# Sobel layers of a four-layer network: products in column halves with 128 rows, and another pipeline order

## The chip, the cores and the metric

The kernel runs on one core of one Trainium2 chip. The metric is the device time of one execution in microseconds (us), lower being better. A core has five engines with a queue each: TensorE (PE in the profile, with its weight loads as PEld), VectorE (DVE), ScalarE (ACT), GpSimd (POOL) and SyncE (SP). Each works its own queue in order and waits at semaphores for the others. SBUF is the working memory of 128 partitions; PSUM[...] takes the products of TensorE.

## The reference

The input `x` has shape (1, 256, 256, 32): height, width, channels, all float32. Four layers are added to it one after the other, each on the group-normed value:

```python
x = x + L0(_gn(x), ...)   # layer norm, then a gated projection
x = x + L1(_gn(x))        # Sobel layer
x = x + L2(_gn(x))        # Sobel layer, the same once more
x = x + L3(_gn(x), ...)   # recurrent cell, 256 steps along the width
```

`_gn` subtracts the mean and divides by the standard deviation over height, width and the two channels of each of 16 groups. A Sobel layer is

```python
pooled = _avg_pool3_same(x)        # 3 x 3 mean over the positions that exist
grad_x = _depthwise3(pooled, kx)   # difference along width, smoothed along height
grad_y = _depthwise3(pooled, ky)   # difference along height, smoothed along width
return jnp.sqrt(grad_x * grad_x + grad_y * grad_y + 1e-6)
```

with Sobel kernels divided by 4 and the same for every channel.

## The kernel before

**Layout.** `xa` and `xb` hold the whole image in SBUF. A partition is a width position inside a group of four times a channel (4 x 32 = 128), the free axis is 64 such groups (`NB`) times 256 heights (`S`). Everything along height is then elementwise work on shifted rows; everything along width is a product with a fixed 128x128 matrix on TensorE. A Sobel layer goes through 32 blocks of two groups (`NST = 32`), so 128 x 512 numbers at a time. The first Sobel layer reads `xa` and writes `xb`, the second goes back.

**One block.** `normalize` (L413, ACT) writes the normed block twice, as `xp` in PSUM and as `xn` in SBUF. `twos` (L420, DVE) adds neighbouring rows to `u`. `threes` (L429, DVE) adds the third row, into `pp`, which is padded by a zero row at each end; `ends` (L423, ACT) writes its two border rows. `fours` (L434, DVE) adds neighbours of `pp` to `v`. `smooth` (L438, POOL) adds neighbours of `v` to `sh`, the smoothed value along height; `difference` (L442, POOL) subtracts rows of `pp` that lie two apart, giving `dh`. Both are rings of eight groups, four blocks deep.

Pooling and Sobel along width together reach two width positions to each side. So a group of four needs itself and half a group on each side. `kt` holds five 128x128 matrices for each of the two gradients: from the group before, from itself, from the group after, and from itself for the first and the last group. `centre` (L449, L459 for the two end blocks) multiplies by the matrix of the group itself; `edges` (L489) adds what comes from the group before (rows 64 to 127 of the ring into columns 0 to 63 of the output) and from the group after (rows 0 to 63 into columns 64 to 127), as 64x64 products. Where the ring wraps, a product of 512 columns is cut in two of 256. Gradient 1 takes `dh`, gradient 0 takes `sh`; they land in the PSUM tiles `pg1` and `pg0`.

`square` (L495, ACT) squares both, gradient 1 in place and gradient 0 into `sq`; `total` (L499, DVE) adds them to `ss`; `root` (L503, ACT) takes the root, back into the PSUM tile of gradient 1; `residual` (L506, DVE) adds the input; `statistics` (L509, DVE) collects the statistics for the next group norm.

**Order.** Nothing here is scheduled by a planner. Each part has a time in a list, `parts`, block k is shifted by `every * k`, the whole list is sorted, and the instructions are emitted in that order. So the times set only the order within each engine's queue; when an instruction starts is up to its queue and its semaphores. Tiles rotate: three PSUM tiles for each gradient, two for `xp`, two SBUF tiles each for `xn`, `u`, `v`, `sq`, `ss`, and two fixed `pp`.

**Beside it.** After the statistics of the first blocks one piece of preparation for the last layer is put in (`between`): in the first Sobel layer reductions on DVE (L641, L645) and 24 subtractions on POOL (L648), in the second a few small products that borrow a `pg1` tile (L660, L669, L675). After each layer `group_norm` (L155 to L174) finishes the statistics, with filler products on TensorE (`junk`, L145). Other lines named below: L333 to L349 belong to the first layer's gate and output projection, L710 to the last layer's preparation, L900 and above to the recurrence.

Of the kernel before, what the change touches and what calls it, by code (L numbers as in the profile page):

```python
# [11 lines left out]
F32 = mybir.dt.float32  # L12
BF16 = mybir.dt.bfloat16
AF = mybir.ActivationFunctionType
# [4 lines left out]
S = 256  # L19
# [3 lines left out]
NB = T // J  # L23
P = 128
# [9 lines left out]
K_GN, K_CEN, K_AVG, K_SOBEL = 0, 1, 2, 3  # L34
# [26 lines left out]
def net_kernel(  # L61
# [20 lines left out]
    nc = tc.nc  # L82
# [15 lines left out]
    kt = cp.tile([P, NK, P], F32, name="kt")  # L98
# [34 lines left out]
    NST = NB // 2  # L133
# [51 lines left out]
    for g in range(4):  # L185
        rows = slice(g * C, (g + 1) * C)
# [9 lines left out]
    with tc.tile_pool(name="nat", bufs=3) as natp, tc.tile_pool(  # L196
        name="ps_in", bufs=4, space=PSUM
    ) as ps_in:
        norm_test(tc, natp, flag, gn_gamma, gn_beta)
        for w0 in range(0, T, WL):  # L200
# [3 lines left out]
            for b2 in range(WL // (2 * J)):  # L204
# [10 lines left out]
                dst = xa[:, blk : blk + 2, :].rearrange("p b s -> p (b s)")  # L215
# [15 lines left out]
    def pair(t, k):  # L231
        return t[:, 2 * k : 2 * k + 2, :].rearrange("p b s -> p (b s)")

    with tc.tile_pool(name="ln", bufs=4) as lnp:
        rstd = lnp.tile([P, 2 * S], F32, name="rstd", bufs=1)
        with tc.tile_pool(name="ps_ln", bufs=6, space=PSUM) as ps_ln, tc.tile_pool(
            name="ps_var", bufs=1, space=PSUM
# [38 lines left out]
        with tc.tile_pool(name="ps_sp", bufs=8, space=PSUM) as ps_sp:  # L276
            for i, (k, g, ks) in enumerate(pairs):
                rows = slice(g * C, (g + 1) * C)
# [3 lines left out]
                    lhsT=spread[rows, ks * J : (ks + 1) * J, :].rearrange("p j c -> p (j c)"),  # L282
                    rhs=rstd[rows, :],
                    start=True,
                    stop=True,
# [19 lines left out]
    with tc.tile_pool(name="at", bufs=3) as atp, tc.tile_pool(  # L305
        name="ps_g", bufs=4, space=PSUM
# [72 lines left out]
    RING = 8  # L379
    Q = P // 2  # L380

    def sobel_layer(src, dst, scale, bias, between):

        stats = new_stats()
        stack = ExitStack()
        kp = stack.enter_context(tc.tile_pool(name="sobk", bufs=1))
        sp = stack.enter_context(tc.tile_pool(name="sob", bufs=2))
        ps_s = stack.enter_context(tc.tile_pool(name="ps_s", bufs=3, space=PSUM))
        ps_c = stack.enter_context(tc.tile_pool(name="ps_c", bufs=2, space=PSUM))

        along = [kp.tile([P, RING, S], F32, name="sh"), kp.tile([P, RING, S], F32, name="dh")]

        pps = [kp.tile([P, 2, S + 2], F32, name=f"pp{i}") for i in range(2)]
        for pp in pps:
            nc.gpsimd.memset(pp[:, :, 0 : S + 2 : S + 1], 0.0)
        v = {}

        def flat(t):
            return t.rearrange("p b s -> p (b s)")

        def ring(k):
            b = 2 * k % RING
            return slice(b, b + 2)

        def normalize(k):
            for key, t in (
                ("xp", ps_c.tile([P, 2, S], F32, name="xp")),
                ("xn", sp.tile([P, 2, S], F32, name="xn")),  # L410
            ):
                v[key, k] = t
                nc.scalar.activation(  # L413
                    flat(t), pair(src, k), AF.Identity, scale=scale, bias=bias
                )

        def twos(k):
            u = v["u", k] = sp.tile([P, 2, S - 1], F32, name="u")
            xn, xp = v.pop(("xn", k)), v["xp", k]
            nc.vector.tensor_add(u, xn[:, :, 0 : S - 1], xp[:, :, 1:S])  # L420

        def ends(k):
            nc.scalar.mul(  # L423
                pps[k % 2][:, :, 1 : S + 1 : S - 1], v["u", k][:, :, 0 : S - 1 : S - 2], 1.5
            )

        def threes(k):
            u, xp = v.pop(("u", k)), v.pop(("xp", k))
            nc.vector.tensor_add(pps[k % 2][:, :, 2:S], u[:, :, 0 : S - 2], xp[:, :, 2:S])  # L429

        def fours(k):
            pp = pps[k % 2]
            w = v["v", k] = sp.tile([P, 2, S + 1], F32, name="v")
            nc.vector.tensor_add(w, pp[:, :, 0 : S + 1], pp[:, :, 1 : S + 2])  # L434

        def smooth(k):
            w = v.pop(("v", k))
            nc.gpsimd.tensor_add(along[0][:, ring(k), :], w[:, :, 0:S], w[:, :, 1 : S + 1])  # L438

        def difference(k):  # L440
            pp = pps[k % 2]
            nc.gpsimd.tensor_sub(along[1][:, ring(k), :], pp[:, :, 0:S], pp[:, :, 2 : S + 2])  # L442

        def centre(k, which):
            pg = v["pg", which, k] = ps_s.tile([P, 2, S], F32, name=f"pg{which}")
            k0 = K_SOBEL + 5 * which
            b = 2 * k % RING
            if 0 < k < NST - 1:
                nc.tensor.matmul(  # L449
                    flat(pg),  # L450
                    lhsT=kt[:, k0 + 1, :],
                    rhs=flat(along[which][:, ring(k), :]),
                    start=True,
                    stop=False,
                )
                return
            for i in range(2):
                m = 3 if 2 * k + i == 0 else 4 if 2 * k + i == NB - 1 else 1
                nc.tensor.matmul(  # L459
                    pg[:, i, :],  # L460
                    lhsT=kt[:, k0 + m, :],
                    rhs=along[which][:, b + i, :],
                    start=i == 0,
                    stop=False,
                )

        def edges(k, which):

            pg = v["pg", which, k]
            k0 = K_SOBEL + 5 * which  # L470
            sides = []
            for m, first, rows, cols in (
                (0, 2 * k - 1, slice(Q, P), slice(0, Q)),
                (2, 2 * k + 1, slice(0, Q), slice(Q, P)),
            ):
                blocks = [(n, n - first) for n in (first, first + 1) if 0 <= n < NB]
                parts = []
                if len(blocks) == 2 and (first + 1) % RING:
                    b = first % RING
                    parts.append((flat(along[which][rows, b : b + 2, :]), flat(pg[cols])))  # L480
                else:
                    for n, i in blocks:
                        parts.append((along[which][rows, n % RING, :], pg[cols, i, :]))
                sides.append([(kt[rows, k0 + m, cols], rhs, out) for rhs, out in parts])
            while any(sides):
                for side in sides:
                    if side:
                        w, rhs, out = side.pop(0)
                        nc.tensor.matmul(out, lhsT=w, rhs=rhs, start=False, stop=not side)  # L489

        def square(k, which):
            pg = flat(v["pg", which, k])
            sq = pg if which else sp.tile([P, 2 * S], F32, name="sq")
            v["sq", which, k] = sq
            nc.scalar.activation(sq, pg, AF.Square)  # L495

        def total(k):
            ss = v["ss", k] = sp.tile([P, 2 * S], F32, name="ss")
            nc.vector.tensor_add(ss, v.pop(("sq", 0, k)), v["sq", 1, k])  # L499

        def root(k):
            mag = v["mag", k] = v.pop(("sq", 1, k))
            nc.scalar.activation(mag, v.pop(("ss", k)), AF.Sqrt, bias=sobel_eps)  # L503

        def residual(k):
            nc.vector.tensor_add(pair(dst, k), pair(src, k), v.pop(("mag", k)))  # L506

        def statistics(k):
            nc.vector.bn_stats(stats[:, k, :], pair(dst, k))  # L509

        every = 4.0
        parts = [
            (-1.45, normalize, ()),
            (0.0, twos, ()),
            (0.66, ends, ()),
            (0.66, threes, ()),
            (1.32, fours, ()),
            (1.4, difference, ()),
            (2.05, smooth, ()),
            (2.6 + 4.0, centre, (1,)),  # L520
            (3.46 + 4.0, centre, (0,)),
            (0.3 + 8.0, edges, (1,)),
            (1.35 + 8.0, edges, (0,)),
            (1.5 + 8.0, square, (1,)),
            (2.5 + 8.0, square, (0,)),
            (3.2 + 8.0, total, ()),
            (0.0 + 12.0, root, ()),
            (1.98 + 12.0, residual, ()),
            (2.6 + 12.0, statistics, ()),
        ]  # L530
        todo = [
            (k * every + when, k, part, args) for k in range(NST) for when, part, args in parts
        ]
        todo.sort(key=lambda e: e[:2])
        with tc.manual_schedule():
            for _, k, part, args in todo:
                part(k, *args)
                if part is statistics and between:
                    between.pop(0)(lambda: flat(ps_s.tile([P, 2, S], F32, name="pg1")))
        stack.close()  # L540
        return stats
# [202 lines left out]
class RecurrentInputs:  # L744
# [33 lines left out]
    def of(self, t, rows):  # L778
# [12 lines left out]
        m=0.300, sq=1.814, rd=1.883, pw=2.686, tg=4.187, sf=4.207, so=4.930, fc=5.023,  # L791
# [3 lines left out]
        m=4.328, sq=5.425, rd=6.234, pw=8.247, sf=8.370, tg=8.501, si=8.549, fc=8.711,  # L795
# [297 lines left out]
```

## Time and profile before

| What | us |
|---|---|
| Median of three runs (2629.62 to 2633.8) | 2632.47 |
| The profiled execution, its own time | 2632.46 |
| Its span in the trace, first to last instruction | 2630.6 |
| First Sobel layer, first `xp` to end of the last statistics | 326.0 to 469.9 |
| Second Sobel layer, the same | 475.3 to 617.65 |
| Busy in the span: PE / DVE / ACT / POOL | 2574.9 / 2329.4 / 2296.4 / 1298.0 |

The page gives for each engine its busy time and for each group of instructions the count and mean. The timeline lists single instructions: start, duration, engine, line, operation, the tile written and those read, the shape; in brackets the idle time before it and what ended it. A product in float32 shows up as two records, each with its weight load. Two instructions of one engine may overlap in the trace, since the next one starts while the last one drains; so what an instruction costs in a full queue is the distance of starts, not the duration.

### The profile page before, as it was taken

The page shows a single profiled execution, that of the slowest core. Times are in us where ns is not written, and L with a number is a line of the kernel's source. Part 1 is how long each engine was busy: PE and PEld are TensorE (multiplying, and loading weights), DVE is VectorE, ACT ScalarE, POOL GpSimd, SP SyncE. Part 2 cuts the span into 40 slices and gives each one's busy share as a digit, 9 for nine tenths or more (in the row PEclk, how much of TensorE's full clock was granted, in tenths as well). Part 3 has the DMA queues.
Part 4 walks back from the last instruction along what each step waited for, and adds up shares of the span by engine and source line. Part 5 has one row for each costly group of instructions (what it writes and reads, how often), then busy time and mean ns, then how long its engine had stood idle before and what let it go on. Part 6 is the DMA issues. An engine that isn't in the chain of part 4 may idle for free.

```text
span 2630.6 us, 43062 instructions
## 1 busy us (share of the span) xinstructions
PE 2574.9 (98%) x11181; PEld 1007.4 (38%) x11181; DVE 2329.4 (89%) x6735; ACT 2296.4 (87%) x6948; POOL 1298.0 (49%) x1288
## 2 busy tenths in 40 slices
PE   7999999998999999999999999999999999999997
PEld 4533433433333333333333333333333333333332
DVE  6788799796999999999999999999999999999996
ACT  5677677675999999999999999999999999999996
POOL 2211276463555555555555555555555555555553
PEclk9899999999999999999999999999999999999998
DMA  4000000002010000001010101010000001000000
GB/s 146 1 1 1 18 1 1 0 1 49 1 25 8 18 12 14 16 10 20 6 21 5 21 5 21 5 24 9 18 12 14 16 10 20 6 5 5 5 5 10
DMA packets 110744, 38.68 MB, mean 15 GB/s; under 512 B 74852, under 2 KB 107653, under 8 KB 110488
## 3 DMA queue, kind: packets, MB, share of 16 engines
q1 hardware_dynamic: 108452, 34.54, 6.1%
q8 instruction: 92, 1.51, 0.3%
q14 instruction: 164, 1.34, 0.2%
q10 hardware_dynamic: 1236, 0.99, 0.1%
q0 software_dynamic: 800, 0.30, 0.1%
HBM read 10.63 MB, written 8.39 MB: 7 GB/s over the span
## 4 chain that ended last, share of the span: by engine, by line
PE 93%; DVE 3%; ACT 2%; POOL 1%; issue 1%; DMA 1%; DVEq 0%; SPq 0%; ACTq 0%; POOLq 0%
PE zz L911 35%; PE zz L906 16%; PE zz L879 8%; PE pt L963 6%; PE pv L315 5%; PE pg L489 4%; PE pg L449 3%; PE zz L876 3%; PE pg L339 2%; PE pt L959 2%; PE pg L315 1%; PE px L1008 1%; PE pc L259 1%; PE px L998 1%; PE pb L280 1%
## 5 line engine op out<-in xcount | busy, mean ns | idle before, releaser
L927 POOL TENSOR_TENSOR rs<-ve,mhalf 128x4 f32<-128x4 f32 x1024 | 1047.1, 1023 | 953.5 <-DVE ve L924 953.5
L911 PE MATMUL zz<-wc,hT 128*128 128x512 f32 x2040 | 1069.0, 612 | 1.4 <-DVE hT L969 1.2
L900 ACT ACTIVATE ga<-zz,rs 128x128 f32<-128x128 f32 x3072 | 974.7, 376 | 53.6 <-POOL rs L927 47.3
L924 DVE TENSOR_REDUCE ve<-sq 128x4 f32<-128x516 f32 x1024 | 705.2, 689 | 69.4 <-ACT sq L919 49.1
L919 ACT ACTIVATE sq<-zz 128x512 f32<-128x512 f32 x1024 | 623.7, 609 | 53.8 <-PE zz L911 14.2
L906 PE MATMUL zz<-wc,hT 128*128 128x512 f32 x1024 | 524.4, 594 | 0.0
L911 PEld LDWEIGHTS zz<-wc,hT 128*128 128x128 f32 x2040 | 306.7, 189 | 355.8 <-DVE hT L969 168.7
L900 ACT ACTIVATE go<-zz,rs 128x128 f32<-128x128 f32 x1024 | 394.1, 385 | 0.0
L947 DVE TENSOR_TENSOR c<-ga 128x128 f32<-128x128 f32 x1024 | 298.4, 291 | 65.1 <-ACT ga L900 58.6
L951 DVE TENSOR_TENSOR fc<-ga,c 128x128 f32<-128x128 f32 x1020 | 297.9, 292 | 5.5 <-ACT ga L900 4.1
L955 DVE TENSOR_TENSOR c<-c,fc 128x128 f32<-128x128 f32 x1020 | 286.7, 281 | 8.8
L879 PE MATMUL zz<-fx,xt 32*128 32x512 f32 x2048 | 265.8, 589 | 0.0
L333 DVE TENSOR_TENSOR o<-pv,sg 128x512 f32<-128x512 f32 x256 | 158.1, 681 | 43.3 <-PE pg L315 37.7
L959 PEld LDWEIGHTS pt<-ident,go 128*128 128x128 f32 x512 | 71.1, 139 | 290.8 <-ACT go L900 283.4
L906 PEld LDWEIGHTS zz<-wc,hT 128*128 128x128 f32 x1024 | 172.7, 209 | 9.4 <-issue 9.4
L963 PEld LDWEIGHTS pt<-ident,c 128*128 128x128 f32 x512 | 70.9, 139 | 268.9 <-DVE c L955 260.9
L966 ACT ACTIVATE th<-c 128x128 f32<-128x128 f32 x512 | 166.0, 324 | 4.6 <-DVE c L955 1.2
L963 PE MATMUL pt<-ident,h 128*128 128x128 f32 x512 | 157.9, 308 | 10.8 <-DVE h L973 8.5
L330 ACT ACTIVATE sg<-pg 128x512 f32<-128x512 f32 x256 | 138.6, 599 | 31.0 <-PE pg L315 26.3
L966 ACT ACTIVATE th<-pt 128x128 f32<-128x128 f32 x512 | 146.2, 286 | 18.9 <-PE pt L963 18.9
L969 DVE TENSOR_TENSOR hT<-pt,th 128x128 f32<-128x128 f32 x512 | 144.1, 282 | 13.8 <-ACT th L966 13.8
L315 PE MATMUL pv<-xb,wv 32*128 32x512 f32 x512 | 156.2, 619 | 0.0
(169 smaller groups left out, 2991.6 us busy)
## 6 DMA issues: line engine op xcount, KB each, us to landing
xt<-xa SPq DMA_DIRECT2D x256, 64.0 KB, 2.0
nat<-in_x_dram SPq DMA_DIRECT2D x16, 512.0 KB, 7.1
out_dram<-st SPq DMA_DIRECT2D x252, 32.0 KB, 1.7
wc<-in_L_conv_W_cell_dram SPq DMA_DIRECT2D x2, 512.0 KB, 4.8
kt<-in_consts_dram ACTq DMA_DIRECT2D x1, 832.0 KB, 6.1
wv<-in_L_conv_Wv_dram POOLq DMA_DIRECT2D x4, 32.0 KB, 4.2
wg<-in_L_conv_Wg_dram POOLq DMA_DIRECT2D x4, 32.0 KB, 6.2
out_dram<-st ACTq DMA_DIRECT2D x4, 32.0 KB, 3.3
```

The source lines that it names most:

```text
L315: nc.tensor.matmul(ps, lhsT=w[rows, half * P : (half + 1) * P], rhs=mn, start=True, stop=True)
L879: nc.tensor.matmul(v["zz", l, h, t], lhsT=inputs.of(t, r), rhs=fx[r, :], start=False, stop=l == 0 and t == 0,)
L900: nc.scalar.activation(dst, gates(x, g), func, scale=scale)
L906: nc.tensor.matmul(get("zz"), lhsT=v["hT", 0, t][:, seqs], rhs=wc[:, l, 0, :], start=False, stop=t == 0)
L911: nc.tensor.matmul(get("zz"), lhsT=v["hT", l, t - 1][:, seqs], rhs=wc[:, l, 1, :], start=False, stop=True,)
L919: nc.scalar.activation(sqs[l, h][:, :, 0:H], four(get("zz")), AF.Square, scale=float(H**-0.5))
L924: nc.vector.tensor_reduce(ve, sqs[l, h], AX.X, ALU.add)
L927: nc.gpsimd.tensor_tensor(rs, get("ve"), inputs.mhalf, ALU.pow)
L947: nc.vector.tensor_mul(c, gates(get("ga"), 0), gates(get("ga"), 2))
L951: nc.vector.tensor_mul(fc, gates(get("ga"), 1), get("c"))
L963: nc.tensor.transpose(get("pt")[:, 1, 0:P], get("c" if turned else "h"), ident)
L966: nc.scalar.activation(th, get("pt")[:, 1, 0:P] if turned else get("c"), AF.Tanh)
```

## The change

`normalize` becomes `convert`, called twice, with times of its own for `xp` and `xn`. `centre` and `edges` become `mixed`: the output of a block is made in two halves of 64 columns, each by two products with all 128 rows: the left half from the group before and the group itself, the right half from the group itself and the group after. The two halves alternate in TensorE's queue. The matrices are the same; the rows that the 64x64 products left out hold zeros in them. The list of times is new, with 3.65 in place of 4.0 between blocks. All other parts are as they were.

```diff
-        def centre(k, which):
-            pg = v["pg", which, k] = ps_s.tile([P, 2, S], F32, name=f"pg{which}")
...
-                    lhsT=kt[:, k0 + 1, :],
-                    rhs=flat(along[which][:, ring(k), :]),
...
-        def edges(k, which):
...
-            for m, first, rows, cols in (
-                (0, 2 * k - 1, slice(Q, P), slice(0, Q)),
-                (2, 2 * k + 1, slice(0, Q), slice(Q, P)),
-            ):
...
+        def mixed(k, which):
+
             pg = v["pg", which, k] = ps_s.tile([P, 2, S], F32, name=f"pg{which}")
             k0 = K_SOBEL + 5 * which
             sides = []
+            for side in range(2):
+                cols = slice(side * Q, (side + 1) * Q)
                 parts = []
+                for d in (side - 1, side):
+                    m = 1 + d
+                    blocks = [n for n in (2 * k + d, 2 * k + 1 + d) if 0 <= n < NB]
+                    whole = len(blocks) == 2 and (blocks[0] + 1) % RING
+                    if whole and (d or 0 < k < NST - 1):
+                        b = blocks[0] % RING
+                        parts.append((kt[:, k0 + m, cols], flat(along[which][:, b : b + 2, :]), flat(pg[cols])))
+                        continue
+                    for n in blocks:
+                        end = 3 if n == 0 else 4 if n == NB - 1 else 1
...
+                sides.append(parts)
+            count = [len(parts) for parts in sides]
             while any(sides):
+                for i, side in enumerate(sides):
                     if side:
+                        w, rhs, dst = side.pop(0)
+                        first = len(side) == count[i] - 1
+                        nc.tensor.matmul(dst, lhsT=w, rhs=rhs, start=first, stop=not side)
...
-        every = 4.0
+        every = 3.65
         parts = [
-            (-1.45, normalize, ()),
-            (0.0, twos, ()),
-            (0.66, ends, ()),
-            (0.66, threes, ()),
-            (1.32, fours, ()),
-            (1.4, difference, ()),
-            (2.05, smooth, ()),
-            (2.6 + 4.0, centre, (1,)),
-            (3.46 + 4.0, centre, (0,)),
-            (0.3 + 8.0, edges, (1,)),
-            (1.35 + 8.0, edges, (0,)),
-            (1.5 + 8.0, square, (1,)),
-            (2.5 + 8.0, square, (0,)),
-            (3.2 + 8.0, total, ()),
-            (0.0 + 12.0, root, ()),
-            (1.98 + 12.0, residual, ()),
-            (2.6 + 12.0, statistics, ()),
+            (-1.19, convert, ("xp",)),
+            (-0.74, convert, ("xn",)),
+            (0.00, twos, ()),
+            (0.52, ends, ()),
+            (1.98, threes, ()),
+            (3.36, difference, ()),
+            (3.62, fours, ()),
+            (5.32, smooth, ()),
+            (8.70, mixed, (1,)),
+            (9.90, mixed, (0,)),
+            (12.45, square, (1,)),
+            (12.47, square, (0,)),
+            (13.90, total, ()),
+            (14.41, root, ()),
+            (15.59, residual, ()),
+            (16.31, statistics, ()),
         ]
```

Sorted, the list gives DVE the order `pp`, `ss`, `v`, `u`, `xb` (residual), `stats` in every step, where it had `pp`, `v`, residual, `stats`, `ss`, `u`. `ss` then belongs to a block three behind that of `pp`, the residual to one four behind that of `u` when it comes.

More of the change, by code (lines that the diff above doesn't have):

```diff
@@ L403, in ring, with convert @@
             return slice(b, b + 2)
[L407 to L410, printed above, removed]
-            ):
[L412 to L415, printed above, removed]
+        def convert(k, key):
+            t = (ps_c if key == "xp" else sp).tile([P, 2, S], F32, name=key)
+            v[key, k] = t
+            nc.scalar.activation(flat(t), pair(src, k), AF.Identity, scale=scale, bias=bias)
         def twos(k):
@@ L442, in difference @@
             nc.gpsimd.tensor_sub(along[1][:, ring(k), :], pp[:, :, 0:S], pp[:, :, 2 : S + 2])
-        def centre(k, which):
+        def mixed(k, which):
             pg = v["pg", which, k] = ps_s.tile([P, 2, S], F32, name=f"pg{which}")
             k0 = K_SOBEL + 5 * which
[L447 to L450, printed above, removed]
-                    lhsT=kt[:, k0 + 1, :],
-                    rhs=flat(along[which][:, ring(k), :]),
[L453 to L465, printed above, removed]
@@ L467, in edges @@
-        def edges(k, which):
-            pg = v["pg", which, k]
-            k0 = K_SOBEL + 5 * which
-            sides = []
-            for m, first, rows, cols in (
-                (0, 2 * k - 1, slice(Q, P), slice(0, Q)),
-                (2, 2 * k + 1, slice(0, Q), slice(Q, P)),
-            ):
-                blocks = [(n, n - first) for n in (first, first + 1) if 0 <= n < NB]
-                parts = []
[L478 to L484, printed above, removed]
+            sides = []
@@ new lines, in mixed @@
+            for side in range(2):
+                cols = slice(side * Q, (side + 1) * Q)
+                parts = []
+                for d in (side - 1, side):
[8 more added lines that the diff above has]
+                        end = 3 if n == 0 else 4 if n == NB - 1 else 1
+                        parts.append(
+                            (
+                                kt[:, k0 + (m if d else end), cols],
+                                along[which][:, n % RING, :],
+                                pg[cols, n - d - 2 * k, :],
+                            )
+                        )
+                sides.append(parts)
@@ L485, in edges @@
+            count = [len(parts) for parts in sides]
             while any(sides):
-                for side in sides:
+                for i, side in enumerate(sides):
                     if side:
-                        w, rhs, out = side.pop(0)
-                        nc.tensor.matmul(out, lhsT=w, rhs=rhs, start=False, stop=not side)
+                        w, rhs, dst = side.pop(0)
+                        first = len(side) == count[i] - 1
+                        nc.tensor.matmul(dst, lhsT=w, rhs=rhs, start=first, stop=not side)
```

## The prediction

> **What bounds the kernel now.** I read the page first, then windows by stage, then the timelines of VectorE (DVE) and GpSimd (POOL) over one step of a Sobel layer. On the page the last layer's cell fills most of the span; the change touches only the two Sobel layers. The source view dates these: first `xp` at 326.0 and last statistics ending at 469.9 us in the first (143.9 us), 475.3 to 617.65 in the second (142.3 us). The windows view of a steady stretch of the second:
>
> ```profile
> core 0: us, PE busy (x) PEld busy (x) DVE busy (x) ACT busy (x) POOL busy (x), PEclk, DMA share, GB/s
> 570.00:602.00 32.00, 32.00 (x112) 11.94 (x110) 29.95 (x48) 25.12 (x47) 19.88 (x16) 1.00 0.00 1
> ```
>
> PE looks full and DVE 94% full, but a busy PE need not be at its peak. So I look at starts. One step on DVE:
>
> ```profile
> 404.38 0.68 DVE L429 TENSOR_TENSOR pp<-u,xp 128x508 f32<-128x508 f32 x1
> 405.20 0.70 DVE L434 TENSOR_TENSOR v<-pp 128x514 f32<-128x514 f32 x1
> 405.81 0.68 DVE L506 TENSOR_TENSOR xb<-xa,pg 128x512 f32<-128x512 f32 x1
> 406.53 0.69 DVE L509 BATCH_NORM_STATS2 stats<-xb 128x6 f32<-128x512 f32 x1
> 407.14 0.67 DVE L499 TENSOR_TENSOR ss<-sq,pg 128x512 f32<-128x512 f32 x1
> 407.73 0.68 DVE L420 TENSOR_TENSOR u<-xn,xp 128x510 f32<-128x510 f32 x1
> 408.51 0.68 DVE L429 TENSOR_TENSOR pp<-u,xp 128x508 f32<-128x508 f32 x1
> ```
>
> The columns are start, duration, engine, line. From `pp` to `pp` is 4.13 us, and every start follows from the one before. An instruction that doesn't need its predecessor starts some 0.08 us before that one ends (0.59 to 0.61 after its start); one that does need it starts later: `u` to `pp` 0.78, `pp` to `v` 0.82, residual to statistics 0.72. Sum: 0.82+0.61+0.72+0.61+0.59+0.78 = 4.13. **The order on DVE sets the step.** PE starts `dh` centre, `sh` centre, `dh` edges, `sh` edges 0.96, 0.95 and 0.91 us apart (404.72, 405.68, 406.63, 407.54); with about 0.91 for the last it needs 3.73 and then waits for `sh` (release by POOL). ACT's starts need some 3.2 of 4.13. POOL:
>
> ```profile
> 405.25 1.55 POOL L442 TENSOR_TENSOR dh<-pp 128x512 f32<-128x512 f32 x1 [0.42 <-DVE pp L429]
> 406.76 1.03 POOL L438 TENSOR_TENSOR sh<-v 128x512 f32<-128x512 f32 x1
> ```
>
> `dh` starts just behind `v` (0.04 to 0.05 us) and takes 1.55. In the filling of the pipeline, `v` comes while `sh` runs:
>
> ```profile
> 333.13 1.03 POOL L438 TENSOR_TENSOR sh<-v 128x512 f32<-128x512 f32 x1
> 333.90 0.81 DVE L434 TENSOR_TENSOR v<-pp 128x514 f32<-128x514 f32 x1
> ```
>
> This `v` ends 0.55 after `sh` ends (334.71 against 334.16); so do the three others that began inside an `sh` (331.50, 480.83, 483.23). And in the steady state `dh` always ends 0.90 after `v` ends. They take turns.
>
> **What the Trainium skill says.** "SBUF — State Buffer", section Who interferes with whom: a DVE instruction with two SBUF inputs and a GpSimd instruction that reads SBUF exclude each other; whoever is first holds the port, the other blocks. `v` is the only one of the six with two SBUF inputs (`pp` twice; the others read PSUM or one tensor). The 0.55 and 0.90 above agree. "TensorEngine Tiling (Array Packing)", section Tiling Modes: 128x64 gives two independent tiles, and a change of mode drains TensorE. The trace shows column tiles with 128 rows side by side: L339 puts 32 records of 128x32 into 3.64 us, 0.43 for four, and L710 (33 rows, 64 columns) shows pairs 0.43 to 0.48 apart. "VectorE: DVE Perf Modes", section The DRAIN you can't avoid, says that a semaphore costs nothing extra between DVE instructions; here the dependent ones cost 0.11 to 0.22 more, and the trace decides.
>
> **The change, part by part.** Measured against the profiled execution: 2632.46 us, span 2630.6, equal to the median of the runs shown (2632.47). Edits cost as follows.
>
> 1. *Products.* Per step and gradient, one 128x128 product and a pair of 64x64 go; two pairs of 128x64 come. Each logical fp32 product leaves two records, so 12 records become 16, on wrap steps a few more. A pair costs 0.86 (2 x 0.43) to 0.96: PE needs 3.44 to 3.84. In a step over 4.1 that is hidden: it costs nothing, under a faster DVE up to 0.1 a step. The last pair waits for `dh` or `sh` of the next step as the edges do now.
>
> 2. *ACT and the other queues.* The two conversions part in name only. ACT keeps its order (root, ends, squares, `xp`, `xn`), with squares and root one block further behind: about 3.2 of work in any step over 3.7, so no cost. Its squares come out some 0.6 us before `total` needs them, its `xn` well before `u`. POOL keeps its order too (`dh`, `sh`, then in 11 steps of the first layer two weight subtractions of 1.18 together, which in a long step end at 0.5 after the next `pp` starts, before `dh` can run). SP and the DMAs get nothing new.
>
> 3. *DVE order.* In place of pp, v, residual, statistics, ss, u comes pp, **ss**, v, u, residual, statistics. With free spacings: pp to ss 0.60, ss to v 0.59, v to u 0.61, u to residual 0.60, residual to statistics 0.72, statistics to pp 0.61: 3.73, so 0.40 would be won in each step.
>
> 4. *But POOL now comes first.* `dh` needs only `pp`: it starts 0.86 after `pp` starts (405.25 less 404.38, and in neighbouring steps the same). `v` used to start 0.82 after `pp`, just ahead; now `ss` stands between and `v` starts 0.60+0.59 = 1.19 after. How soon does `dh` take the port? Alone it should last 1.25 to 1.27: two late `dh` (397.29 and 536.75) lasted so, and the addition L349 of the same size takes 1.27 from idle. Of this 0.90 lies behind the port's release, so it claims the port 0.36 after its start or, if `v` releases somewhat before its end, 0.26: at 1.12 to 1.22. `v` claims between its start and its stream (0.15 later): 1.19 to 1.34. I take POOL as first, narrowly. Then `dh` ends at 0.86+1.26 = 2.12, `v` at 2.12+0.55 = 2.67, `u` starts at 2.59, and the step is 2.59+0.60+0.72+0.61 = **4.52**, 0.39 more than now. Lower bound: if `dh` alone lasts only 1.03, as `sh` does, 4.29. Behind the blocked `v` stand `u` and all of DVE, and `sh` on POOL; PE has 0.7 and ACT over 0.6 spare, so nothing else is late next.
>
> 5. *Both ends of a layer.* Four blocks instead of three enter before the first square. Following the queues from the first `xp`, the fifth `pp` starts at 14.1 us (second layer; first 15.3 with two reductions) instead of 16.3 (17.45): 2.1 won. The emptying, 11.9 from the last `pp`, gains the late `v` and becomes some 12.4: 0.5 lost. The second layer now spends 114.13 us on 27 steps and two extra additions, 1.4 more than 27 x 4.13 + 1.2; most of this wait for PSUM tiles of the side products should go, since a slower step gives PE slack: 1 won.
>
> Sum: 2 x (27 x 0.39 - 2.1 + 0.5) - 1 = +16.9; with 4.51 from the shorter `dh` of 1.25, +16.3. I take +15.5, shaded towards the lower bound, so **2648 us**; its own range is 2641 to 2653 with the two lengths of `dh` weighed. The recurrence isn't touched.
>
> **Rivals.** *Short block:* `dh` alone is 1.03, the step 4.29. Sum 2 x (27 x 0.16 - 2.1 + 0.4) - 1 = +4, that is 2636: within what can't be told. For it: `sh` lasts 1.03. Against: `sh` always runs straight behind `dh`, its dispatch hidden; L349 doesn't.
>
> *`v` wins the port:* at the tie of part 4, if `v` claims at its start (1.19) and `dh` only at 1.22, `dh` is the one that blocks, as now, and the step is 3.73, or up to 3.84 if pairs cost 0.96 on PE. Sum: 2 x (27 x (-0.40) - 2.1 - 0.2) + 1 = -25, or -19 with the slower PE: 2607 to 2613. It decides from the point at which `dh` claims later than `v`. It is self-sustaining, since POOL is through with `sh` well before the next `pp` ends. For it: a margin of 0.1 us at most. Against: of the range of claims most is on POOL's side.
>
> *The halves don't run side by side:* eight products at 0.86 make 6.9 us of PE a step, some 170 us in all. L339 speaks against it.
>
> **How the numbers follow.** A measurement here can tell some 0.2% (5.3 us) from no change. Long block 0.47 (slower); short block 0.17 (0.07 of it beyond 0.2%); `v` wins 0.27 (faster); a mixture of steps of both kinds 0.06 (0.04 same, 0.02 faster); PE halves in turn or another new wait 0.03 (slower). So faster 0.29, same 0.14, slower 0.57. The predicted time is that of the long block. As it holds hardly half, the range has to reach the rival of the other sign: 2608 to 2652.
>
> **What would show it.** Right: DVE's `v` at about 1.25 to 1.5 us instead of 0.70, ending 0.55 after `dh`; `dh` at 1.03 to 1.27 instead of 1.55; `pp` to `pp` at 4.3 to 4.5. Wrong: `v` still 0.70 and `dh` 1.55 with a step of 3.7 to 3.85 (`v` first), or PE records of 64 columns 0.86 apart one by one. An earlier fifth `pp` by 2 us tests part 5. If the layers keep their 143.9 and 142.3 us, the step is right by accident or the order was not the bound.

## The result, and the profile after

The changed kernel takes 2634.8 us (median of 20 runs, 2632.46 to 2636.78) against 2632.43 us before on the same chip (20 runs, 2629.62 to 2638.96). The ratio is **1.0006**, with a 95% interval of 1.0 to 1.0013: 0.06%, inside the 0.2% named as what can't be told from no change. The forecast was 2648 us. The profiled execution after has a span of 2631.7 us (before 2630.6).

In the traces the two Sobel layers are where the change acts. The first lasts 144.9 us instead of 143.9, the second 143.8 instead of 142.3. Of these 2.4 us the two profiled executions win some back elsewhere: 0.8 between the layers, and what follows the second takes 2012.2 instead of 2013.0. By stages:

| us | first layer before | after | second layer before | after |
|---|---|---|---|---|
| first `xp` to fifth `pp` | 17.45 | 15.3 | 16.3 | 14.4 |
| fifth to last `pp` (27 steps) | 114.57 | 117.56 | 114.13 | 117.42 |
| last `pp` to the end | 11.92 | 12.04 | 11.92 | 12.04 |

So the layers fill 2 us sooner, and lose 3.0 and 3.3 us again in the steady part. The windows view of the same stretch as before (start and end, length, then busy time of each engine with the instruction count) says who is now busy all the time:

```profile
570.00:602.00 32.00, 28.54 (x135) 10.58 (x134) 31.76 (x46) 23.39 (x44) 15.98 (x16) 1.00 0.00 1
```

PE fell from 32.00 to 28.54, DVE rose from 29.95 to 31.76 of 32 us though it issued two instructions fewer: the time for which an instruction is blocked counts as busy. One step on DVE, from the timeline of after:

```profile
353.80 0.67 DVE L424 TENSOR_TENSOR pp<-u,xp 128x508 f32<-128x508 f32 x1
354.39 0.68 DVE L481 TENSOR_TENSOR ss<-sq,pg 128x512 f32<-128x512 f32 x1
354.98 1.25 DVE L429 TENSOR_TENSOR v<-pp 128x514 f32<-128x514 f32 x1
356.16 0.67 DVE L415 TENSOR_TENSOR u<-xn,xp 128x510 f32<-128x510 f32 x1
356.75 0.68 DVE L488 TENSOR_TENSOR xb<-xa,pg 128x512 f32<-128x512 f32 x1
357.46 0.69 DVE L491 BATCH_NORM_STATS2 stats<-xb 128x6 f32<-128x512 f32 x1
358.07 0.67 DVE L424 TENSOR_TENSOR pp<-u,xp 128x508 f32<-128x508 f32 x1
```

The starts lie 0.59, 0.59, 1.18, 0.59, 0.71 and 0.61 us apart, 4.27 in all (before 4.13). Five of the six are the spacings of the prediction's part 3 (the 0.71 is the statistics directly behind the residual that they read); `v` alone is long, 1.25 us where it took 0.70. POOL in the same step:

```profile
354.65 1.04 POOL L437 TENSOR_TENSOR dh<-pp 128x512 f32<-128x512 f32 x1 [0.35 <-ACT xp L410]
356.38 1.04 POOL L433 TENSOR_TENSOR sh<-v 128x512 f32<-128x512 f32 x1 [0.69 <-DVE v L429]
```

`dh` starts 0.85 us after `pp` (354.65 less 353.80; 0.83 to 0.85 in the other regular steps), ahead of `v`, and lasts **1.04 us** where it took 1.55. It ends at 355.69; `v` ends at 356.23, 0.54 later. (The bracket names `xp`, which ended at 354.53, 0.06 after `pp`. But `difference` reads only `pp`, and in e3, where `xp` ended 0.19 before `pp`, `dh` starts at the same 0.84 after `pp`.) `sh` then waits for `v`. The source view shows that this is the common case (count, then shortest/median/longest in ns); of the 64 `dh`, 55 last 1.03 to 1.06:

```profile
L429 DVE TENSOR_TENSOR v<-pp x64: 677/1248/1542, 329.4 to 608.6; 128x514 f32<-128x514 f32 x64
L437 POOL TENSOR_TENSOR dh<-pp x64: 1033/1040/1934, 329.4 to 608.3; 128x512 f32<-128x512 f32 x64
```

### The profile page after: what moved, and what is told of

It reads as the page before. It is cut to its first block, busy times and chain, and to the rows that moved or that the text cites. A ratio compares the mean times of both kernels' runs of the same rounds, so it can differ in the third digit from the quotient of the medians.

```text
span 2631.7 us, 43547 instructions
## 1 busy us (share of the span) xinstructions
PE 2553.0 (97%) x11453; PEld 1004.5 (38%) x11453; DVE 2348.0 (89%) x6735; ACT 2291.8 (87%) x6948; POOL 1273.7 (48%) x1288
## 4 chain that ended last, share of the span: by engine, by line
PE 86%; DVE 9%; ACT 2%; issue 1%; DMA 1%; POOL 1%; SPq 0%; DVEq 0%; ACTq 0%; POOLq 0%
PE zz L892 35%; PE zz L887 17%; PE zz L860 8%; PE pt L944 6%; PE pv L315 5%; PE zz L857 3%; DVE v L429 3%; PE pt L940 2%; PE pg L339 2%; DVE stats L491 2%; DVE u L415 1%; PE px L989 1%; PE pg L315 1%; DVE pp L424 1%; PE pc L259 1%
## 5 line engine op out<-in xcount | busy, mean ns | idle before, releaser
L471 PE MATMUL pg<-dh,kt 128*64 128x512 f32 (+1 forms) x584 | 175.8, 544 | 24.9 <-POOL dh L437 24.6
```

## The experiments

The theory: **the new order alone makes the result.** Its other spacings would give a step of some 3.7 us, but it lets `dh` take the port that DVE and GpSimd share ahead of `v`, and `v` pays 0.56 us a step. Rivals: the products in column halves cost or gain something themselves; or `v` is long for another reason than `dh` (its place behind `ss`, its own operands). Each ratio below is to the kernel before, run on the same chip.

### The two parts of the change, each alone

The products alone, under the old list of times:

```diff
-            (2.6 + 4.0, centre, (1,)),
-            (3.46 + 4.0, centre, (0,)),
-            (0.3 + 8.0, edges, (1,)),
-            (1.35 + 8.0, edges, (0,)),
+            (0.3 + 8.0, mixed, (1,)),
+            (1.35 + 8.0, mixed, (0,)),
```

> The new products alone (128-row column halves in place of centre and 64x64 edges), with the old list of times. Theory: DVE's order sets the step, so `pp` to `pp` stays 4.13 us, PE's shorter or longer work is hidden, and the time stays within 2 us of the kernel before (2632). Rival, the products themselves cost (a weight load more per product, 16 records for 12): the step grows and the time is 2637 or more. Rival, they gain by themselves (no change of tile mode): the step falls below 4.1 and the time to 2628 or less. PE's pairs should lie 0.86 to 0.91 us apart if the halves run side by side.

Measured: 2632.44 us, ratio 0.9999 (0.999 to 1.0008). DVE and POOL are as before. From its timeline, `v` and `dh` of one step:

```profile
562.75 0.69 DVE L434 TENSOR_TENSOR v<-pp 128x514 f32<-128x514 f32 x1
562.79 1.55 POOL L442 TENSOR_TENSOR dh<-pp 128x512 f32<-128x512 f32 x1 [1.57 <-DVE pp L429]
```

The order alone, with the old products:

```diff
-            (8.70, mixed, (1,)),
-            (9.90, mixed, (0,)),
+            (8.70, centre, (1,)),
+            (8.71, centre, (0,)),
+            (9.90, edges, (1,)),
+            (9.91, edges, (0,)),
```

> The new list of times alone, with the old products (centre, then edges, where the column halves stand in the changed kernel). Theory: `dh` takes the port ahead of `v`, `v` lasts 1.25 us, the step is 4.27 as in the changed kernel, and the time within 2 us of its 2635. Rival, the old products do not fit into the new order (TensorE changes its tile mode twice a step): the step is longer than 4.3 and the time above 2638.

Measured: 2634.0 us, ratio 1.0007 (1.0 to 1.0013), step 4.26. Its timeline:

```profile
563.65 1.04 POOL L437 TENSOR_TENSOR dh<-pp 128x512 f32<-128x512 f32 x1 [1.49 <-ACT xp L410]
563.99 1.25 DVE L429 TENSOR_TENSOR v<-pp 128x514 f32<-128x514 f32 x1
```

In the first, `v` comes 0.04 us ahead of `dh` and `dh` is long; in the second, `dh` comes 0.34 ahead and `v` is long. The order carries the whole result; the products neither cost nor bring anything that can be told in either order.

### Is it the port? `v` with one input from SBUF

`v` adds `xp` from PSUM instead of the shifted `pp`, `sh` adds `v` to itself; the order is that of after.

```diff
-            nc.vector.tensor_add(w, pp[:, :, 0 : S + 1], pp[:, :, 1 : S + 2])
+            xp = v.pop(("xp", k))
+            nc.vector.tensor_add(w[:, :, 0:S], pp[:, :, 0:S], xp)
```

> The changed kernel in the same order, but `fours` adds `xp` from PSUM to `pp` in place of the neighbouring row of `pp`, and `smooth` adds `v` to itself: the smoothing along height is left out, the amount of work is the same. `v` then has a single SBUF input. Theory of the shared port: `v` lasts about 0.68 and `dh` 1.04 although they overlap, the step falls to 0.58+0.59+0.60+0.59+0.71+0.61 = 3.68, or to what PE needs (3.5 to 3.8): 2 x 27 x 0.5 = 27 us less than the changed kernel, 2604 to 2612. Rival, `dh` and `v` do not exclude each other and the 1.25 comes from elsewhere: `v` stays near 1.2 and the time near 2635.

Measured: 2607.96 us, ratio 0.9907 (0.9888 to 0.9926), step 3.70. POOL's timeline, then DVE's:

```profile
561.33 1.04 POOL L438 TENSOR_TENSOR dh<-pp 128x512 f32<-128x512 f32 x1 [1.49 <-ACT xp L410]
562.50 1.04 POOL L434 TENSOR_TENSOR sh<-v 128x512 f32<-128x512 f32 x1
```

```profile
561.67 0.68 DVE L430 TENSOR_TENSOR v<-pp,xp 128x512 f32<-128x512 f32 x1
```

`dh` (561.33 to 562.37) lies over the whole of `v` (561.67 to 562.35), and neither is longer for it. `v` stands in the same place behind `ss` and in front of `u` as in after. `sh` now reads one view twice, but it starts only after `v`. So it is the second input of `v` from SBUF, as the Trainium skill has it ("SBUF — State Buffer", section Who interferes with whom).

### Giving the port to `v`: `fours` directly behind `threes`

```diff
-            (3.62, fours, ()),
+            (2.40, fours, ()),
```

> The changed kernel with `fours` at 2.40 in place of 3.62, so that DVE has pp, v, ss, u, residual, statistics: `v` waits for `pp` and starts 0.82 after it, ahead of `dh` (0.83 to 0.86). Theory of the shared port: `v` lasts 0.70 again, `dh` 1.55, and the step is 0.82+0.61+0.59+0.60+0.71+0.61 = 3.94, that is 0.32 less than the changed kernel's 4.26; over 2 x 27 steps some 17 us: about 2618. Rival, `v` lasts 1.25 for another reason than `dh` (its place in the queue, its PSUM neighbours): it stays long and the time is 2640 or more, since the wait for `pp` comes on top.

Measured: 2632.96 us, ratio 1.0001 (0.9992 to 1.001). The half on the port is right (`v` 0.69, `dh` 1.55), the time is not: the step is 4.18. DVE's timeline, then the root on ACT:

```profile
562.03 0.67 DVE L424 TENSOR_TENSOR pp<-u,xp 128x508 f32<-128x508 f32 x1
562.83 0.69 DVE L429 TENSOR_TENSOR v<-pp 128x514 f32<-128x514 f32 x1
563.44 0.68 DVE L481 TENSOR_TENSOR ss<-sq,pg 128x512 f32<-128x512 f32 x1
564.04 0.68 DVE L415 TENSOR_TENSOR u<-xn,xp 128x510 f32<-128x510 f32 x1
564.88 0.69 DVE L488 TENSOR_TENSOR xa<-xb,pg 128x512 f32<-128x512 f32 x1 [0.16 <-ACT pg L485]
```

```profile
564.16 0.69 ACT L485 ACTIVATE pg<-ss,sobel_eps 128x512 f32<-128x512 f32 x1 [0.92 <-DVE ss L481]
```

With `v` moved away, only `u` stands between `ss` and the residual that needs its root. `ss` to residual over ACT takes 1.44 us, so DVE now waits 0.16 for the root. And `v` directly behind the `pp` it reads starts 0.80 after it, not 0.6. Step: 0.80 + 0.61 + 1.44 + 0.72 + 0.61 = 4.18. A new wait took the place of the block.

To take that wait away, squares, `total` and root come earlier, so that `ss` runs ahead of `pp`:

```diff
-            (12.45, square, (1,)),
-            (12.47, square, (0,)),
-            (13.90, total, ()),
-            (14.41, root, ()),
+            (11.00, square, (1,)),
+            (11.02, square, (0,)),
+            (12.80, total, ()),
+            (13.30, root, ()),
```

> The changed kernel with `v` directly behind `pp` as in e3, and `ss` moved behind the statistics (squares at 11.00, `total` 12.80, `root` 13.30), so that four DVE instructions lie between `ss` and its residual and the root is ready. Theory: `v` goes ahead of `dh` and lasts 0.70, the residual no longer waits for the root (e3: 0.16 idle each step), and the step is 0.80+0.61+0.60+0.71+0.60+0.58 = 3.90: some 19 us less than the changed kernel, 2616. Rival, the time that e3 did not gain is lost to POOL (1.55 of `dh` plus 1.03 of `sh`) or to PE, not to the root: the step stays at 4.1 to 4.2 and the time at 2630 or more.

Measured: 2665.1 us, ratio 1.0127 (1.011 to 1.0144): a miss, step 4.80. The timeline of all engines:

```profile
563.39 0.69 ACT L485 ACTIVATE pg<-ss,sobel_eps 128x512 f32<-128x512 f32 x1 [1.57 <-DVE ss L481]
...
564.02 0.77 ACT L410 ACTIVATE xp<-xb,bias,scale 128x512 f32<-128x512 f32 x1
...
564.73 0.80 ACT L410 ACTIVATE xn<-xb,bias,scale 128x512 f32<-128x512 f32 x1
...
565.56 0.69 DVE L415 TENSOR_TENSOR u<-xn,xp 128x510 f32<-128x510 f32 x1 [0.78 <-ACT xn L410]
```

The root at 13.30 came to stand ahead of `xp` and `xn` in ACT's queue. It waits for `ss`, everything behind it waits too, and the `u` that needs `xn` waits 0.78. That closes a loop over two engines: `u`, residual, statistics, `ss`, root, `xp`, `xn`, `u`. The starts along it, from the `u` at 560.76 to the one at 565.56, lie 0.61, 0.71, 0.61, 0.70, 0.63, 0.71 and 0.83 apart: the 4.80 of the step. The next run puts the root back to 14.41, behind `xn`, and keeps the rest:

```diff
-            (13.30, root, ()),
+            (14.41, root, ()),
```

> As e7, with `root` back at 14.41. In e7 `root` stood ahead of `xp` and `xn` on ACT, and the trace showed the loop u, residual, statistics, ss, root, xp, xn, u at 4.80 us. Theory: with `root` behind `xn`, the step is the DVE order alone, 0.80+0.61+0.60+0.71+0.60+0.58 = 3.90, 19 us less than the changed kernel: 2614 to 2618, `v` at 0.70 and `dh` at 1.55. Rival: POOL's 1.55 + 1.03 or another loop through ACT holds it at 4.1 or more: 2628 and up.

Measured: 2617.77 us, ratio 0.9953 (0.9936 to 0.9969), step 3.93. DVE and POOL:

```profile
548.94 0.68 DVE L424 TENSOR_TENSOR pp<-u,xp 128x508 f32<-128x508 f32 x1
549.75 0.70 DVE L429 TENSOR_TENSOR v<-pp 128x514 f32<-128x514 f32 x1
```

```profile
549.79 1.56 POOL L437 TENSOR_TENSOR dh<-pp 128x512 f32<-128x512 f32 x1 [1.38 <-ACT pg L485]
```

With the port given to `v` and no wait on ACT, the step is 0.34 shorter than after; the 0.2 above e4's 3.70 is the distance from `pp` to a `v` directly behind it (0.81).

### POOL's reading behind `v`: `sh` ahead of `dh`

The DVE order of after stays; on POOL `sh` comes first, so `dh` finds itself behind the work that needs `v`. Gradient 0 then goes ahead of gradient 1 on PE and ACT.

```diff
-            (3.36, difference, ()),
             (3.62, fours, ()),
-            (5.32, smooth, ()),
-            (8.70, mixed, (1,)),
-            (9.90, mixed, (0,)),
-            (12.45, square, (1,)),
-            (12.47, square, (0,)),
+            (4.30, smooth, ()),
+            (5.32, difference, ()),
+            (8.70, mixed, (0,)),
+            (9.90, mixed, (1,)),
+            (12.45, square, (0,)),
+            (12.47, square, (1,)),
```

> The changed kernel with `smooth` ahead of `difference` on POOL (4.30 and 5.32), and gradient 0 ahead of gradient 1 in products and squares; DVE's order is the changed kernel's. POOL then waits for `v` before it touches `dh`, so nothing of POOL reads while `v` runs. Theory of the shared port: `v` lasts 0.68, `dh` and `sh` 1.04 each, the step is 3.68 (0.58 less), about 27 us less than the changed kernel; in 11 steps of the first layer POOL's weight subtractions reach into the next `v`, up to 2 us back: 2606 to 2611. Rival, `dh` now ends 1.5 to 2 us later in the step and PE, ACT or a ring waits for it: the step is over 3.9 and the time over 2618.

Measured: 2607.07 us, ratio 0.9901 (0.9885 to 0.9918), step 3.70. DVE, then POOL:

```profile
549.44 0.68 DVE L429 TENSOR_TENSOR v<-pp 128x514 f32<-128x514 f32 x1
```

```profile
550.30 1.04 POOL L433 TENSOR_TENSOR sh<-v 128x512 f32<-128x512 f32 x1 [1.66 <-PE pg L471]
551.29 1.04 POOL L437 TENSOR_TENSOR dh<-pp 128x512 f32<-128x512 f32 x1
```

`dh` and `sh` no longer overlap `v` in the regular step, and `v` has its 0.68 again. (In 11 steps of the first layer a weight subtraction, L629, still runs 0.35 us into `v`; `v` isn't longer for it, 0.69.) This median lies 27.7 us below that of after, e4's 26.8 (e4 and e5 ran on different chips, and that of after isn't on record): two ways to take the collision away, at nearly the same gain. That is what it costs, to within the noise.

One spacing is left above 0.6: the statistics directly behind the residual they read (0.71). Moving them behind the next `pp` takes it away:

```diff
-            (16.31, statistics, ()),
+            (16.80, statistics, ()),
```

> As e5_sh_first, with `statistics` at 16.80, so that `pp` stands between the residual and its statistics and no DVE instruction follows the one that it needs. Theory: the step on DVE is 0.60+0.59+0.60+0.59+0.60+0.60 = 3.58, and PE's four pairs need 3.44 to 3.6: 2600 to 2606, some 5 us less than e5_sh_first. Rival, PE is the bound at 3.68 or more: within 1 us of e5_sh_first or behind it.

Measured: 2604.83 us, ratio **0.9893** (0.9877 to 0.991), the lowest median here, though only 2.2 us under e5's on the same chip, which is within what can't be told. In the traces the two layers together last 257.2 us against e5's 263.6. DVE and PE:

```profile
545.43 0.68 DVE L424 TENSOR_TENSOR pp<-u,xp 128x508 f32<-128x508 f32 x1
546.03 0.68 DVE L491 BATCH_NORM_STATS2 stats<-xa 128x6 f32<-128x512 f32 x1
546.63 0.67 DVE L481 TENSOR_TENSOR ss<-sq,pg 128x512 f32<-128x512 f32 x1
547.22 0.68 DVE L429 TENSOR_TENSOR v<-pp 128x514 f32<-128x514 f32 x1
547.82 0.68 DVE L415 TENSOR_TENSOR u<-xn,xp 128x510 f32<-128x510 f32 x1
548.42 0.68 DVE L488 TENSOR_TENSOR xa<-xb,pg 128x512 f32<-128x512 f32 x1
549.02 0.67 DVE L424 TENSOR_TENSOR pp<-u,xp 128x508 f32<-128x508 f32 x1
```

```profile
544.63 2.02 PE L471 MATMUL pg<-sh,kt 128*64 128x512 f32 x8
546.36 2.01 PE L471 MATMUL pg<-dh,kt 128*64 128x512 f32 x8
548.08 2.16 PE L471 MATMUL pg<-sh,kt 128*64 128x512 f32 x8
```

Every DVE instruction follows the last by 0.59 to 0.60 us: 3.59 a step, 0.12 less than e5. PE starts a gradient every 1.72 to 1.73 us, 3.45 of that step. Both engines are nearly full.

### What the products are worth once DVE is out of the way

The two fast orders with the old products, `centre` and `edges` in place of `mixed` (gradient 0 first); first that of e5:

```diff
-            (8.70, mixed, (0,)),
-            (9.90, mixed, (1,)),
+            (8.70, centre, (0,)),
+            (8.71, centre, (1,)),
+            (9.90, edges, (0,)),
+            (9.91, edges, (1,)),
```

> As e5_sh_first, but with the old products (both centres, then both edges). It asks what the column halves are worth once DVE needs only 3.68 a step. Theory: PE needs 0.96+0.95+0.91+0.91 = 3.73 and more on wrap steps, so it becomes the bound and the step is 3.75 to 3.9: 3 to 12 us more than e5_sh_first. Rival, the products don't matter here either: within 2 us of e5_sh_first.

Measured: 2609.46 us, ratio 0.9912 (0.9896 to 0.9929), not to be told from e5's 0.9901: a miss. PE starts the `sh` edges at 544.95, 548.74 and 552.52, so 3.78 to 3.79 apart, where DVE steps by 3.70. It falls back by about 0.08 a step, some 2 us over 27 steps. The slack between the products and the squares takes this up, and the layer pays at its end: from the last `pp` to the end of the layer e6 takes 14.06 and 14.20 us, e5 12.36 in both.

The same edit on the order of e8:

> As e8_sh_first_stats_apart (step 3.58 on DVE, PE's pairs 1.72 a gradient), but with the old products. Theory: centre and edges need 0.96+0.95+0.91+0.91 = 3.73 with no wait at all, so PE now sets the step: 3.73 to 3.8, that is 2 x 27 x 0.15 to 0.22 = 8 to 12 us more than e8, 2613 to 2617. Only here do the column halves pay. Rival, PE's changes of tile mode hide behind other waits: within 3 us of e8.

Measured: 2611.12 us, ratio 0.9918 (0.9901 to 0.9934). The step is not one: in the second layer DVE runs most steps at 3.58 up to the twentieth `pp`, while PE falls back, and from then on at 3.73 to 3.82. PE's timeline over one of the late steps:

```profile
545.98 1.12 PE L444 MATMUL pg<-sh,kt 128*128 128x512 f32 x2
546.94 1.02 PE L444 MATMUL pg<-dh,kt 128*128 128x512 f32 x2
547.89 1.07 PE L484 MATMUL pg<-sh,kt 64*64 64x256 f32 x6
548.81 1.02 PE L484 MATMUL pg<-dh,kt 64*64 64x256 f32 x6
549.76 1.13 PE L444 MATMUL pg<-sh,kt 128*128 128x512 f32 x2
```

The starts lie 0.96, 0.95, 0.92 and 0.95 apart, 3.78, without a gap: here PE sets the step. The two layers last 131.4 and 132.8 us where e8's last 128.3 and 128.9, so the column halves are worth 7.0 us in this order, a little less than expected; 4.2 of it lie behind the last `pp` of the layers. (The two ran on different chips, and the intervals of their ratios overlap slightly; the layers' lengths, from one trace each, are the better measure.)

### How long is `dh` alone, and why is L349 longer?

The forecast took `dh` alone for 1.26, from L349 among others. `dh` reads two views of one tile, L349 two tiles. So `difference` subtracts four rows of `kt` instead:

```diff
-            nc.gpsimd.tensor_sub(along[1][:, ring(k), :], pp[:, :, 0:S], pp[:, :, 2 : S + 2])
+            nc.gpsimd.tensor_sub(along[1][:, ring(k), :], pp[:, :, 0:S], kt[:, 0:4, :].rearrange("p (b k) s -> p b (k s)", b=2))
```

> The changed kernel, but `difference` subtracts four matrices of `kt` from `pp` in place of `pp` two rows on; the difference along height is left out, the sizes are the same. It asks why `dh` alone lasts 1.04 and not the 1.26 of the prediction, which was taken from L349, an addition of two different tiles (1.27). Theory: two views of one tile are read faster than two tiles; `dh` now lasts 1.27, `v` 1.48, the step is 4.26+0.23 = 4.49, and the time 12 us over the changed kernel: 2645 to 2649. Rival, L349 is slow for another reason (in place, long idle before): `dh` stays at 1.04 and the time at 2635.

Measured: 2641.94 us, ratio 1.0037 (1.0024 to 1.0049), step 4.41. POOL and DVE:

```profile
549.85 1.19 POOL L437 TENSOR_TENSOR dh<-pp,kt 128x512 f32<-128x512 f32 x1 [1.49 <-ACT xp L410]
```

```profile
550.19 1.40 DVE L429 TENSOR_TENSOR v<-pp 128x514 f32<-128x514 f32 x1
```

Two tiles cost 0.15 us more (1.19 against 1.04), and `v` again ends 0.55 after `dh` (551.59 against 551.04). The step grows by the same 0.14 to 0.15, and 54 steps of 0.14 make 7.6 us; 7.1 lie between the two medians (the chip of after isn't on record). So the length of `dh` goes into the time one to one. The expected 1.27 was not reached: 0.08 of L349's length stays open (it also writes over its own input, which wasn't tried; nor was it tried whether the rows of `kt`, which lie in memory otherwise than those of `pp`, play a part in the 0.15).

## Why the prediction was wrong in its size, and where it was right

**The step that failed: part 4's "`dh` alone lasts 1.25 to 1.27".** Measured, it is 1.04 from idle. The mechanism was as told: POOL first, `v` blocked, `v` ending 0.55 after `dh`. The length was taken from three pieces of evidence, and each falls.

Two were the late `dh` in the kernel before. Its POOL and DVE timelines for the first of them:

```profile
397.29 1.25 POOL L442 TENSOR_TENSOR dh<-pp 128x512 f32<-128x512 f32 x1 [0.72 <-DVE pp L429]
```

```profile
396.95 0.69 DVE L434 TENSOR_TENSOR v<-pp 128x514 f32<-128x514 f32 x1
```

`v` ends at 397.64 and this `dh` at 398.54, **0.90 later**: the very distance that the prediction gave for blocked `dh`. The one at 536.75 ends at 538.02, 0.91 after the `v` of 536.42 ended at 537.11. They weren't alone. They started 0.33 to 0.34 us behind `v`, while it still had 0.35 to run, so they were blocked for a shorter time. The prediction itself had said that `dh` "always ends 0.90 after `v` ends", and didn't hold this against the two. The third, L349, isn't the same operation: it reads two tiles, which e11 prices at 0.15.

From this the size follows. With 1.04, `dh` ends at 0.83 + 1.04 = 1.87 after `pp`, `v` at 2.42, `u` starts some 0.07 before that, and 2.35 + 0.59 + 0.71 + 0.61 gives 4.26; 4.27 was measured, not 4.52. The prediction's own sum with that step is 2 x (27 x 0.14 - 2.1 + 0.4) - 1 = +3.2; the traces show +2.4 over the two layers (0.9 and 1.5), the medians +2.4. That is the *short block* rival, which had been given 0.17 against the long block's 0.47. Its argument, that `sh` lasts 1.03, was right, and the objection that `sh` starts straight behind `dh`, with its dispatch hidden, was not: from idle `dh` needs 1.04 too.

Point by point:

- **Part 1, products at no cost:** right, by e1 and e2. PE's price is at the low end: 0.86 a pair, 1.72 a gradient in e8. The trace agrees with the two independent tiles that "TensorEngine Tiling (Array Packing)" of the Trainium skill gives in its section Tiling Modes: four records with 128x64 take 0.86 us, and two of the 128x128 form no less. The same section states a drain at a change of mode, and e9's single records fit it. One 128x128 record starts 0.43 after another, also from `sh` to `dh`. The first 64x64 record starts 0.52 after the last 128x128 one, the first 128x128 record 0.52 after the last pair of 64x64 (on steps where the ring doesn't wrap), and the record behind it another 0.53 later. With 0.04 more inside the first edges this makes up the 0.33 by which e9's 3.78 exceeds e8's 3.45. The rival with the halves in turn didn't come; its 170 us would have been nearer 150, 54 times 6.88 less 4.13.
- **Part 2, ACT and the other queues:** right; no wait for ACT shows on DVE in a regular step of after. But e3 and e7 show how close it is: one place further on DVE or ACT, and the root becomes the bound.
- **Part 3, the free order of 3.73:** right; e4 and e5 give 3.70.
- **Part 4, who comes first:** right, with a wider margin than the prediction saw. A `dh` of 1.04 that ends 0.90 after a release claims the port 0.14 after its start (an estimate from these two), 0.98 after `pp`; a `v` of 0.69 that ends 0.55 after a release claims it 0.14 after its own start, which comes only at 1.18. So whichever starts first should have it, and `dh` has a lead of 0.34. The few blocks with a smaller lead bear this out; in after, for one:

```profile
395.93 1.04 POOL L437 TENSOR_TENSOR dh<-pp 128x512 f32<-128x512 f32 x1 [0.63 <-ACT xp L410]
395.97 1.54 DVE L429 TENSOR_TENSOR v<-pp 128x514 f32<-128x514 f32 x1
```

In after, e2 and e11 `dh` had the port in all six blocks in which it led by 0.04 to 0.06 us; the one in which it led by 0.01 (e2) it lost. That `v` might win was given a chance of 0.27, which rested on the same wrong length.

- **Part 5, the ends:** the fifth `pp` came at 15.3 and 14.4 (15.3 and 14.1 predicted), the emptying lost 0.1 in each layer where 0.5 was said. The wait for PSUM tiles in the second layer went from 1.4 to about 0.9 (117.42 less 27 x 4.27 and 1.2), so half of the 1 us that was counted as won.
- **The port as the cause:** right, by e4, which takes away the second SBUF input of `v`, and by e5, which keeps it and takes `dh` out of its way.
- **What a dependence costs on DVE:** that a semaphore costs nothing extra, as "VectorE: DVE Perf Modes" of the Trainium skill has it in its section The DRAIN you can't avoid, isn't what is seen here between an instruction and the reader directly behind it: moving the statistics one place away from the residual won 0.12 us a step (e8).

## What to carry to other kernels

Where an order on DVE is changed, look not only at the distances of starts on DVE but at which GpSimd instruction becomes ready ahead of a DVE instruction with two inputs in SBUF: what was left of `dh` and 0.55 us more then stood in DVE's queue, while the reverse order cost only the engine with time to spare (e1, e10). Put the GpSimd work that depends on that instruction first and the independent reader behind it, and keep an instruction one place away from the one it reads. Before a duration is taken as that of an operation alone, hold its end against the ends of whatever could have blocked it.

## What was not expected of the hardware

- A GpSimd subtraction of 128x512 in float32 takes 1.04 us with both inputs in one tile and 1.19 with two tiles (e11); the in-place addition L349, with two tiles as well, takes 1.27.
- Between `v` and `dh` a lead of 0.04 us was enough to have the port, either way, and the prices of the two orders differ. With `v` ahead by 0.04 us, POOL's `dh` goes from 1.04 to 1.55 and DVE loses nothing (e1). With `dh` ahead by 0.34, DVE's `v` goes from 0.69 to 1.25 and POOL's `dh` loses nothing (e2). Other pairs have other numbers: the weight subtraction of 128x128, which reads one tensor (L629), with a lead of 0.13, held `v` only until 0.31 after its own end (0.78 instead of 0.68, eight steps of e8). And the 128x128 addition into `e` had the port with a lead of 0.02 in e10 and lost it with 0.05 in e9.
- A blocked DVE instruction still lets its successor start some 0.07 us before it ends, as an unblocked one does: `u` 1.18 after a `v` of 1.25.
